# A transformer block with cross-attention: the written-out order of all instructions and the places of its buffers are replaced

## The chip, the cores and the metric

The kernel runs on one core of a Trainium2 chip. The metric is the device time of one execution in microseconds, with all inputs and the output in device memory. Three runs of the kernel before took 652.02, 652.84 and 654.86 us, a median of 652.84.

## The reference

Eight sequences of 256 tokens with 512 features each attend to eight contexts of the same size, with 16 heads of 32 features. All values are f32. A multilayer perceptron with 2048 inner features and the tanh form of gelu follows.

```
x = layer_norm(hidden_states, ln1_w, ln1_b)
q = (x @ q_w + q_b)                      # and split into 16 heads of 32
k = (encoder_hidden_states @ k_w + k_b)
v = (encoder_hidden_states @ v_w + v_b)
scores = where(mask, q k^T / sqrt(32), lowest)
out = softmax(scores) v
hidden = out @ cproj_w + cproj_b + hidden_states
y = gelu(layer_norm(hidden, ln2_w, ln2_b) @ fc_w + fc_b)
return hidden + y @ proj_w + proj_b
```

## The kernel before

The 2048 tokens are worked on in two groups of 1024; a digit 0 or 1 behind a letter in a name (`k1_0`, `o0_1`, `x1`) is the group. The stages of a group are: load and transpose the context (L692-L770); normalise the tokens (`layer_norm`, L793); project to k, v and q (`keys_of`, `values_of`); 16 attention units, one for two head groups and a sequence (`scores` at L1020 and `attend` at L1067); the output projection (`output`, L1410); the multilayer perceptron (`fc`, L1194, and `proj`, L1258).

Every large product is a Strassen-Winograd quad (`quad`, L852): seven products P1, P2, P6, P7, P5, P3, P4 of quarter matrices replace eight. They are written into three PSUM banks called X, Y and W, and between the products another engine reads a bank out (t1, c11, t2, t3, c22, c12, c21). So `k1_0_P7` is the seventh product of the first half of the keys of group 1, and its destination is the bank `k1_0_W`. The sums of quarters that go in (`c1t1`, `kws1`, `fw0i4_1` and so on) are made by VectorE or POOL. All matmuls but the transposes are recorded on one line, L634, so the tile names tell them apart.

An attention unit such as 022 goes like this. TensorE writes the scores s022 into four PSUM banks. ScalarE copies them out in eight pieces (ev022, line L614, tile `pr`), VectorE takes maxima (mx022, L1033), ScalarE moves these together (mc022, L1039), VectorE folds and transposes them (L1040 and mf022, L1042). The result is stored to device memory (md022) and loaded back, broadcast to all partitions (mm022). VectorE (L1053) or POOL (L1057) subtracts it from the two halves of the scores (less022_0, less022_1), ScalarE takes exponentials (L1060), for half of the units VectorE or POOL adds the exponentials in pairs (`ss`, L625), and TensorE multiplies with the values (av022). VectorE inverts the sums (L1083-L1086) and writes the result (att022, L625), which frees the bank of av022.

Nothing in this order is decided while the kernel runs or by a planner in the file. `Order.op` (L54) records each operation with the engines that it may run on and finds what it depends on. `Order.run` (L94) then reads the sequence of issue on all engines from a string, PROGRAM, of 2999 words; a letter behind a word names the engine where there is a choice (V VectorE, A ScalarE, G POOL). Each engine issues its own words in this sequence and never overtakes. All transfers are on the queue of SyncE, also in this sequence, and a transfer that waits for its data holds up those behind it. A second string, PLACES, gives each buffer its slot:

```
for word in PROGRAM.split():
    name, _, e = word.partition(":")
    o = ops.pop(name)
    o.eng = letters[e] if e else o.alts[0][0]
    o.start = len(order)
    order.append(o)
...
where = dict(p.split("=") for p in PLACES.split())
for o in order:
    for b in o.bufs:
        if b.slot is None and b.name in where:
            b.slot = int(where[b.name])
```

The slots are 45 pieces of 1024 f32 for each partition (a piece can serve as two of 512), 14 pieces of 256, small ones, and the eight PSUM banks (kinds W and C). A buffer waits until all users of the one before it in the same slot are done.

Of the kernel before, what the change touches and what calls it, by code (L numbers as in the profile page):

```python
# [122 lines left out]
cq0_00_0 turn_c0_10_0 turn_c0_00_0 vw00 c0_10_0:A c0_00_0:V small v0_0_P1a cq0_00_1 turn_c0_00_1 c0_00_1:A cq0_01_1  # L123
turn_c0_10_1 v0_0_P1b c0_10_1:V v0_1_P1a cq0_01_0 turn_c0_11 cq0_11_0 c0_11:V vw10 cq0_11_1 kw00 vw11 v0_0_t1:A
turn_c0_01 cq0_10_0 cq0_10_1 c0_01:V c0t1:V v0_1_P1b v0_1_t1:A rows1 vws1:V turn_c0_31 turn_c0_21 vws3:G c0_21:A rows7
vws2:G c0_31:A k0_1_P1 xt0_3 vw01 k0_0_P1 rows3 turn_c0_20 c0t2:V fw0_11_0 v0_0_P6 stats_x0_11 c0t3:V vws4:V rows0
turn_c0_30 fw0_11_1 fw0i4_1:G v0_0_t2:A xt0_2 aggr_x0_11 rows2 v0_1_P6 stats_x0_10 c0_20:A aggr_x0_10 kw10 v0_0_P5
rows5 c0_30:A eps_x0_1 v0_0_P2 rows4 rows6 fw0_10_0 c0t4:V v0_1_t2:V v0_0_t3:A pow_x0_1 nb_x0_1 norm_x0_11:A mk kw11
rows8 v0_1_P2 fw0_00_1 v0_0_P3 kws3:V mk~1 fw0i4_3:G fw0_10_1 cols fw0_00_0 xt0_5 v0_1_P5 fw0i4_2:V xt0_6 fw0i4_4:V
kws1:V kws2:V cols~1 k0_0_t1:A k0_1_t1:V xt0_0 k0_1_P6 v0_0_c11 xt0_7 fw0_01_0 fw0s3:V v0_1_t3:A xt0_1 fw0s1:G  # L130
fw0i5_1:G v0_1_c11 stats_x0_31 k0_0_P7 stats_x0_21 k0_1_t2:A fw0i5_2:G kw01 xt0_4 fw0_01_1 fcd0_5_False fcd0_7_False
stats_x0_00 fw0i5_3:V fw0i1_1:V fcd0_4_True fw0i7_1:G fw0i1_3:V k0_0_P6 qw00 k0_0_t2:A aggr_x0_00 fw0i7_2:V fw0i7_4:V
v0_1_P3 fw1_01_0 k0_1_P2 k0_0_P5 fw0i1_2:V fw0s2:V norm_x0_10:A aggr_x0_21 fw1_00_0 qw11 aggr_x0_31 fw0i5_4:V qw01
fw0i1_4:V k0_1_P5 vd0_0_11 stats_x0_01 aggr_x0_01 fw1_01_1 eps_x0_0 v0_1_c12:A kws4:G fw0i7_3:V v0_0_c12:A stats_x0_20
# [12 lines left out]
aggr_x1_11 fold000 q0_1_P5 cb1_00 s020 fw1i5_2:G cb1_02 cb1_13 q0_1_c11 fw1i4_2:V q0_1_t3:A cb1_21 mf000 fw1i3_4:V
q0_1_P3 ev020_21 ev020_20 q0_0_P3 fw1i5_3:G ev020_01 fcd0_3_True eps_x1_1 ev020_30 cb1_10 fw1i7_2:V ev020_31 fw1i5_4:V
fw1i6_1:V ev020_11 mx020_1 ev020_10 ev020_00 fw1i7_3:V fw1i6_2:G mx020_0 q0_1_c12:A q0_1_P7 cT1_10 q0_0_c12:A
fw1i4_4:G cb1_22 fcd1_3_False md000 mc020_2 cT1_00 cT1_11 mc020_1 mc020_3 kd0_0_12 fcd1_7_False pow_x1_1 s002  # L150
fcd1_4_True ev002_10 ev002_11 fold020 mm000 ev002_30 ev002_31 ev002_21 ev002_20 fw1i7_4:V ev002_01 mf020 fw1i3_3:G
v0_0_P7 ev002_00 cT1_01 s022 kd0_1_11 nb_x1_1 v0_1_P7 fw1i6_3:G q0_1_c22 fw1i6_4:G mx002_1 q0_1_P4 fcd1_3_True
ev022_20 mx002_0 v0_1_c22 c1t1:G ev022_30 ev022_21 ev022_31 mx022_1 md020 ev022_10 less000_0:G less000_1:G v0_0_c22
cb1_20 mc002_3 ev022_01 mc002_1 mc002_2 fold002 fcd1_6_False v0_1_P4 ev022_11 mm020 q0_1_c21 v0_1_c21 mf002 ev022_00
v0_0_P4 mx022_0 exp000_0 norm_x1_11:A s010 mc022_3 mc022_1 k1_0_P1 exp000_1 cb1_33 cb1_30 cb1_32 mc022_2 ss000_0:G
cT1_20 cb1_31 v0_0_c21 ev010_30 ev010_11 md002 less020_1:V ev010_00 ev010_21 fold022 ev010_01 ev010_31 fcd1_5_True
ev010_20 ss000_1:G k1_1_P1 kd0_1_22 cT1_21 mf022 ev010_10 less020_0:V av000 s030 exp020_0 cT1_31 cT1_30 norm_x1_10:A
fcd1_6_True md022 k1_1_t1:A xt1_7 ev030_21 ev030_01 mx010_1 ev030_30 xd1_3 r000 att000 k1_0_P2 mx010_0 ev030_00
k1_0_t1:A c1t2:G k1_1_P6 exp020_1 ev030_31 ev030_20 ev030_11 k1_0_c11 mc010_1 mc010_2 mc010_3 c1t3:G kd0_1_12
ss020_0:V ev030_10 kd0_1_21 mm022 xt1_4 k1_0_P6 k1_0_t2:A ss020_1:V xt1_0 av020 stats_x1_31 mx030_1 mx030_0 aggr_x1_31  # L160
fold010 k1_1_t2:A s012 xt1_6 stats_x1_30 ev012_21 fcd1_7_True mc030_2 mc030_1 ev012_31 xt1_1 r020 k1_1_P5 stats_x1_01
att020 mf010 k1_0_P5 mm002 mc030_3 aggr_x1_30 xd1_2 kd0_0_22 k1_0_P7 less022_1:G exp022_1 md010 less022_0:G
stats_x1_00 ev012_20 exp022_0 ss022_0:V ev012_01 vd0_0_21 ku011 less002_1:V ev012_00 k1_0_t3:A mm010 less002_0:V
ev012_30 ev012_11 ev012_10 aggr_x1_01 k1_1_t3:A fold030 vd0_0_12 ss022_1:G av022 c1t4:G exp002_0 s032 vu010 xt1_5
vu030 ev032_30 ev032_11 mf030 aggr_x1_00 k1_0_c22 mx012_1 vd0_1_11 k1_1_P3 ev032_10 ev032_20 ss002_0:G mx012_0 k1_0_P3
ku001 ev032_01 ev032_31 eps_x1_3 eps_x1_0 ev032_00 less010_1:V exp002_1 k1_1_P7 ss002_1:G k1_0_P4 ev032_21 mx032_1
exp010_1 k1_0_c12:A mx032_0 vd0_0_22 stats_x1_20 av002 mc032_2 md030 mc032_3 ku021 mc032_1 k1_0_c21 r022 fold032
att022 mf032 k1_1_c12:A ku003 pow_x1_0 r002 mc012_1 s001 stats_x1_21 mc012_3 att002 k1_1_P2 less010_0:G ss010_1:G
exp010_0 vu011 nb_x1_0 mm030 k1_1_c22 ss010_0:G ev001_11 aggr_x1_21 ev001_31 vu012 pow_x1_3 ev001_30 md032 vu032 ku031
ev001_00 ev001_01 ev001_21 aggr_x1_20 av010 ev001_10 ev001_20 s021 ku023 k1_1_c11 k1_1_P4 norm_x1_01:A eps_x1_2  # L170
# [182 lines left out]
cq0_00=74 cq0_10=32 cq0_01=88 cq0_11=40 ps_cols=7 ps_c0_00_0=6 c0_00=58 ps_c0_00_1=0 ps_c0_10_0=2 ps_c0_10_1=6  # L353
ps_c0_20=7 c0_10=48 ps_c0_30=2 ps_c0_01=2 c0_01=20 ps_c0_11=1 ps_c0_21=2 c0_11=24 ps_c0_31=7 xt0_0=54 xt0_1=6 xt0_2=77
# [105 lines left out]
ps_o11=0 ot1=28 ps_o01=4 ps_o10=7  # L460
# [1053 lines left out]
```

## Time and profile before

| | before |
|---|---|
| median of three runs | 652.84 us (652.02 to 654.86) |
| the profiled execution: its span | 652.0 us (no other time of it is recorded) |
| TensorE, busy | 644.3 us, 99%, 3793 matmuls |
| VectorE, busy | 583.2 us, 89% |
| ScalarE, busy | 346.1 us, 53% |
| POOL, busy | 395.9 us, 61% |
| transfers, share of 16 engines' time | 78.0% |
| granted TensorE clock | 1.000 |

Rows of the profile are read thus. PE is TensorE, DVE is VectorE, ACT is ScalarE, SPq is SyncE's queue, on which a transfer is issued; its data land later. A row of the timeline gives the start, the length, the engine, the line, the operation, the tile written and the tiles read, and in square brackets how long the engine was idle before it and what ended that. Names of tiles are given without their numbers: a buffer in a shared slot can appear under the name of the slot's first user, such as `vw` or `xt`. Matmul ends are modelled, so a stretch that reads as fully busy may hold small gaps.

### The profile page before, as it was taken

Reading aid. Unit: us, or ns where it says so; the run is one execution under the profiler, and the core shown is the slowest. Engines: PE = TensorE matmul, PEld = TensorE weight load, DVE = VectorE, ACT = ScalarE, POOL = GpSimd, SP = SyncE. Lnnn points to the kernel's source line nnn. Section 1 sums busy time; section 2 is a strip of 40 time slices with the busy share of each in tenths; the row PEclk is TensorE's granted clock in tenths of the full one; section 3 lists DMA queues with packets and bytes.
Section 4 is the critical chain, followed back from the end, with each engine's and each line's share of the span. In section 5 each row is a group of like instructions: output and inputs, shape, how many; then the busy total and the mean of one; then the engine's idle time right before and its main releaser. Section 6 shows DMA issues by size and latency. Waiting matters only on the chain.

```text
span 652.0 us, 11225 instructions
## 1 busy us (share of the span) xinstructions
PE 644.3 (99%) x3793; PEld 487.7 (75%) x3793; DVE 583.2 (89%) x985; ACT 346.1 (53%) x709; POOL 395.9 (61%) x351
## 2 busy tenths in 40 slices
PE   9999999999999999999999999999999999999997
PEld 7755463477545776777787888888888888888886
DVE  4989998999999999999999999988878777999975
ACT  2244698999999879966864645220121222523000
POOL 2543675879987897898859756335813265321244
PEclk9999999999999999999999999999999999999999
DMA  8999998778875447787867787897989989677765
GB/s 268 306 328 324 239 251 284 226 204 152 217 224 151 130 168 232 260 267 250 257 214 250 225 272 232 293 314 170 160 222 197 215 198 204 158 190 227 173 138 97
DMA packets 206713, 144.83 MB, mean 222 GB/s; under 512 B 117136, under 2 KB 167104, under 8 KB 206656
## 3 DMA queue, kind: packets, MB, share of 16 engines
q1 hardware_dynamic: 206656, 144.11, 78.0%
q8 instruction: 30, 0.49, 0.3%
q14 instruction: 27, 0.22, 0.1%
HBM read 104.10 MB, written 39.98 MB: 221 GB/s over the span
## 4 chain that ended last, share of the span: by engine, by line
PE 90%; DVE 4%; ACT 2%; issue 1%; DMA 1%; POOL 1%; DVEq 0%
PE pd_X L634 15%; PE fc_X L634 15%; PE fc_W L634 7%; PE pd_W L634 7%; PE av L634 6%; PE q_X L634 4%; PE v_X L634 4%; PE fc_Y L634 4%; PE k_X L634 4%; PE pd_Y L634 4%; PE s L634 4%; PE o_X L634 2%; PE v_W L634 2%; PE k_W L634 2%; PE o_W L634 2%; DVE mx L1033 2%
## 5 line engine op out<-in xcount | busy, mean ns | idle before, releaser
L614 ACT ACTIVATE pr<-s,cols 128x256 f32<-128x256 f32 x256 | 102.9, 485 | 10.7 <-PE s L634 8.2
L1057 POOL TENSOR_TENSOR pr<-pr,mm 128x512 f32<-128x512 f32 x70 | 90.2, 1318 | 7.2 <-DMA xt<-in_x_dram 5.0
L1237 ACT ACTIVATE h<-h,cols 128x256 f32<-128x256 f32 x128 | 55.2, 499 | 61.2 <-DVE h L625 45.2
L1033 DVE TRANSPOSE_TENSOR_REDUCE mx<-pr 128x32 f32<-128x1024 f32 x64 | 76.9, 1216 | 1.5 <-ACT pr L614 1.3
L1060 ACT ACTIVATE pr<-pr 128x1024 f32<-128x1024 f32 x64 | 66.5, 1061 | 12.1 <-POOL pr L1057 9.0
L625 DVE TENSOR_TENSOR h<-fc_X,h 128x512 f32<-128x512 f32 x80 | 52.4, 675 | 5.5 <-PE fc_X L634 4.7
L625 POOL TENSOR_TENSOR ss<-pr 128x512 f32<-128x512 f32 x24 | 31.5, 1325 | 14.2 <-ACT pr L1060 11.8
L625 DVE TENSOR_TENSOR h<-fc_W,h 128x512 f32<-128x512 f32 x48 | 32.0, 677 | 5.0 <-PE fc_W L634 4.4
L1053 DVE TENSOR_TENSOR pr<-pr,mm 128x1024 f32<-128x1024 f32 x29 | 35.2, 1229 | 0.0
L1039 ACT COPY mx<-mx 32x64 f32<-32x64 f32 x96 | 23.2, 243 | 15.9 <-DVE mx L1033 14.7
L623 POOL TENSOR_TENSOR z1t<-h,z1t 128x512 f32<-128x512 f32 x6 | 8.0, 1360 | 26.1 <-PE pd_Y L634 12.3
L625 POOL TENSOR_TENSOR tq<-tq,rq 128x512 f32<-128x512 f32 x8 | 10.1, 1272 | 21.7 <-DMA rq<-hd 15.4
L634 PE MATMUL pd_X<-z0i,pl 128*128 128x256 f32 x96 | 22.5, 379 | 0.0
L634 PE MATMUL fc_W<-y1i,fl 128*128 128x256 f32 x84 | 20.7, 379 | 0.0
L625 DVE TENSOR_TENSOR h<-fc_Y,h 128x512 f32<-128x512 f32 x24 | 15.9, 672 | 5.3 <-PE fc_Y L634 5.3
L634 PE MATMUL pd_W<-z1i,pl 128*128 128x256 f32 x88 | 20.6, 379 | 0.0
L1040 DVE TENSOR_REDUCE mx<-mx 32x32 f32<-32x256 f32 x32 | 18.4, 578 | 2.2 <-ACT mx L1039 2.0
L634 PEld LDWEIGHTS pd_X<-z0i,pl 128*128 128x128 f32 x96 | 18.2, 190 | 2.5
L811 POOL TENSOR_TENSOR rs_y<-rs_y,neg_half 128x2 f32<-128x2 f32 x8 | 10.2, 1289 | 15.3 <-DMA pl<-prd 7.7
L634 PE MATMUL pd_X<-h,pl 128*128 128x256 f32 x80 | 18.9, 379 | 0.0
L601 ACT COPY h<-fc_X 128x512 f32<-128x512 f32 x16 | 9.0, 594 | 18.5 <-PE fc_X L634 15.6
L625 DVE TENSOR_TENSOR po<-pd_X,po 128x256 f32<-128x256 f32 x24 | 9.9, 414 | 9.6 <-PE pd_X L634 9.4
(574 smaller groups left out, 1857.3 us busy)
## 6 DMA issues: line engine op xcount, KB each, us to landing
pl<-prd SPq DMA_DIRECT2D x65, 256.0 KB, 3.7
mm<-md SPq DMA_DIRECT2D x32, 512.0 KB, 4.3
fl<-fcd SPq DMA_DIRECT2D x40, 256.0 KB, 4.5
fw<-in_L_xattn_fc_w_dram SPq DMA_DIRECT2D x16, 256.0 KB, 4.0
hid<-in_x_dram SPq DMA_DIRECT2D x8, 512.0 KB, 5.8
pw<-in_L_xattn_proj_w_dram SPq DMA_DIRECT2D x32, 128.0 KB, 4.1
hd<-hid SPq DMA_DIRECT2D x8, 512.0 KB, 4.9
fcd<-fw0i SPq DMA_DIRECT2D x7, 512.0 KB, 7.1
```

The source lines that it names most:

```text
L601: (nc.scalar.copy if e == "ACT" else nc.vector.tensor_copy)(to(), of_())
L614: lambda e: nc.scalar.activation(to(), of_(), AF.Identity, bias=bias(), scale=1.0))
L625: E[e].tensor_tensor(to(), in0(), in1(), op)
L634: nc.tensor.matmul(o(), l(), r(), start=first, stop=True, skip_group_check=True)
L811: lambda e, rs=rs: nc.gpsimd.tensor_tensor(tile_of(rs)[:, 2:4], tile_of(rs)[:, 0:2], neg_half[:, 0:2], ALU.pow), lock=True)
L1033: T.op(f"mx{u}_{h}", [("DVE", 1.126)], [(pr[h], None)], [(mx, [h])], lambda e, h=h: nc.vector.tensor_reduce(tile_of(mx)[:, 0:64].rearrange ...
L1039: lambda e, a=a: nc.scalar.copy(tile_of(mx)[0:32, 64 * a : 64 + 64 * a], tile_of(mx)[32 * a : 32 * a + 32, 0:64]))
L1040: T.op(f"fold{u}", [("DVE", 0.38)], [(mx, [0, 1, 2, 3, 4])], [(mx, [5])], lambda e: nc.vector.tensor_reduce(tile_of(mx)[0:32, 256:288], ti ...
L1053: nc.vector.tensor_tensor(p_, p_, m_[:, None, :].to_broadcast([P, 2, 512]), ALU.subtract)
L1057: E[e].tensor_tensor(p_, p_, m_, ALU.subtract)
L1060: lambda e, h=h: nc.scalar.activation(tile_of(pr[h]), tile_of(pr[h]), AF.Exp), table="exp")
L1237: lambda e, f=f, b=b, c=c: nc.scalar.activation(at(h[f][b], c), at(h[f][b], c), AF.Gelu_apprx_tanh, bias=col(c_fcb + f * 4 + c), scale=1.0 ...
```

## The change

Only the two strings differ. PROGRAM has the same 2999 operations in another sequence on every engine, and 167 operations stand on another one of their allowed engines: of the words with a letter, VectorE has 252 instead of 261, POOL 270 instead of 254, ScalarE 134 instead of 141. PLACES gives 1029 of 1304 buffers another slot or bank. No operation is added or removed, and the code that makes the instructions is the same.

```diff
--- before.py
+++ after.py
@@ -120,344 +120,344 @@
 PROGRAM = """
-cq0_00_0 turn_c0_10_0 turn_c0_00_0 vw00 c0_10_0:A c0_00_0:V small v0_0_P1a cq0_00_1 turn_c0_00_1 c0_00_1:A cq0_01_1
...
-ss020_0:V ev030_10 kd0_1_21 mm022 xt1_4 k1_0_P6 k1_0_t2:A ss020_1:V xt1_0 av020 stats_x1_31 mx030_1 mx030_0 aggr_x1_31
...
-att020 mf010 k1_0_P5 mm002 mc030_3 aggr_x1_30 xd1_2 kd0_0_22 k1_0_P7 less022_1:G exp022_1 md010 less022_0:G
...
-ev132_11 ev132_30 ev132_31 o0_0_c12 exp102_0 o0_1_t3 ev132_01 fold112 pw0_10_11 exp122_1 o0_0_P7 att100 mf112 mm130
...
+cq0_00_0 small turn_c0_10_0 turn_c0_00_0 c0_00_0:V cq0_00_1 vw00 turn_c0_00_1 turn_c0_10_1 c0_10_0:A v0_0_P1a
...
+mx010_1 r000 k1_1_t1:A exp020_0 exp020_1 c1t2:G k1_0_c11 c1t3:G mm022 less022_1:G k1_1_P6 k1_0_P6 norm_x1_10:A
...
+k1_0_P7 mc030_1 less002_0:V k1_0_t3:A exp002_0 k1_1_P5 xt1_1 stats_x1_01 md010 xt1_4 ss022_1:G av022 vu030 mm010 xt1_5
...
+ev132_00 ev132_10 md130 md110 pw0_11_01 mm130 pw0_10_11 o0_0_P7 mx132_0 less120_0:G ev132_31 ev132_20 ev132_30 o0_1_P7
...
 """
...
 PLACES = """
...
-mm010=4 ss010=4 av020=3 r020=1 rc020=4 att0_10=88 vu030=10 s030_0=3 s030_1=5 s030_2=6 s030_3=4 pr030_0=8 pr030_1=10
...
-c1t4=24 x1t1=6 x1t2=66 x1t3=48 x1t4=46 k1_0_X=2 k1_0_11=35 k1_0_Y=7 k1_0_21=65 k1_0_W=3 k1_0_22=41 k1_0_12=60 k1_1_X=1
...
-rc122=1 att1_11=48 s132_0=1 s132_1=0 s132_2=5 s132_3=7 pr132_0=4 pr132_1=66 mx132=2 mm132=80 av110=1 r110=3 rc110=3
...
-o0_0_X=6 o0_0_Y=1 o0_0_W=7 o0_1_X=4 o0_1_Y=5 o0_1_W=2 st_y0_0=2 mv_y0_0=0 rs_y0_0=9 xn_y0_00=68 xn_y0_01=38 st_y0_1=3
...
+mm010=4 ss010=4 av020=5 r020=6 rc020=0 att0_10=88 vu030=3 s030_0=5 s030_1=3 s030_2=0 s030_3=7 pr030_0=8 pr030_1=10
...
+c1t4=24 x1t1=14 x1t2=62 x1t3=50 x1t4=46 k1_0_X=2 k1_0_11=35 k1_0_Y=6 k1_0_21=65 k1_0_W=7 k1_0_22=41 k1_0_12=60
...
+rc122=0 att1_11=48 s132_0=3 s132_1=0 s132_2=7 s132_3=1 pr132_0=4 pr132_1=6 mx132=0 mm132=82 av110=6 r110=8 rc110=7
...
+o0_0_X=4 o0_0_Y=3 o0_0_W=5 o0_1_X=6 o0_1_Y=1 o0_1_W=3 st_y0_0=5 mv_y0_0=3 rs_y0_0=9 xn_y0_00=81 xn_y0_01=11 st_y0_1=9
...
 """
```

Three places show what the strings do. The first is on TensorE, in the key projection of group 1, round unit 022. All rows are matmuls; `s012` are scores of another unit. Before:

```order
L634 MATMUL s012_3_1107<-q0_1_21_742,qw00_460 128x256
L634 MATMUL k1_1_X_985<-c1t1_900,kws1_405 128x512 x2
L634 MATMUL k1_0_X_956<-c1t1_900,kws1_405 128x512 x2
L634 MATMUL k1_0_W_1142<-c1t3_1062,xt0_3_297 128x512 x2
L634 MATMUL av022_1176<-ss022_1154,ones_89 32x256 x4
L634 MATMUL av022_1176<-pr022_0_909,v0_0_22_369 32x256 x2
```

After the change:

```order
L634 MATMUL s012_3_1119<-q0_1_21_747,xt0_5_517 128x256
L634 MATMUL k1_0_X_990<-c1t1_906,kws1_343 128x512 x2
L634 MATMUL k1_0_W_1168<-c1t3_1057,kws1_343 128x512 x2
L634 MATMUL k1_1_X_999<-c1t1_906,kws1_343 128x512 x2
L634 MATMUL av022_1182<-ss022_1160,ones_89 32x256 x4
L634 MATMUL av022_1182<-pr022_0_883,xt0_7_378 32x256 x2
```

The product `k1_0_W` (P7) stood last ahead of av022, and now stands one product earlier, with `k1_1_X` behind it. The table of places moves `k1_0_W` from bank 3, which av020 holds until att020 is done, to bank 7; av020 moves to bank 5, where av022 is as well.

The second place is SyncE's queue, from the stores of the maxima of units 002 and 022 (md, read from mx) to the broadcast load mm022. The other rows are copies of weights sums, keys and tokens (fcd, kd, xd) to device memory and loads of keys and tokens. Before:

```order
L594 DMA md002_146<-mx002_891 32x32
L594 DMA fcd1_5_106<-fw1i5_752 128x2x512
L594 DMA kd0_1_22_127<-v0_0_22_369 128x512
L594 DMA fcd1_6_107<-fw1i6_804 128x2x512
L594 DMA md022_147<-mx022_906 32x32
L588 DMA k1_1_11_1025<-in_x_dram 128x512
L594 DMA xd1_160<-xn_x1_11_940 128x512
L594 DMA kd0_1_12_125<-qw00_460 128x512
L594 DMA kd0_1_21_126<-k0_1_21_440 128x512
L588 DMA mm022_1070<-md022_147 128x1024
```

After the change:

```order
L594 DMA xd1_160<-xn_x1_11_957 128x512
L588 DMA xt1_6_980<-in_x_dram 128x512
L594 DMA kd0_1_12_125<-xt0_5_517 128x512
L588 DMA v0_1_21_335<-in_x_dram 128x512
L594 DMA md022_147<-mx022_922 32x32
L588 DMA ku011_1005<-kd0_1_11_124 128x256
L594 DMA md002_146<-mx002_891 32x32
L594 DMA fcd1_3_104<-fw1i3_856 128x2x512
L588 DMA mm022_1060<-md022_147 128x1024
```

The store md022 now stands ahead of md002 instead of behind it, and another set of transfers stands between it and mm022.

The third place is TensorE in the output projection of group 0. `o0_0` and `o0_1` are the two halves, s132 the scores of a unit of group 1. Before:

```order
L634 MATMUL s132_3_2482<-qws2_639,xn_x1_11_940 128x256
L634 MATMUL o0_1_X_2299<-ows1_1955,a0t1_2284 128x256 x4
L634 MATMUL o0_1_W_2510<-xt0_7_419,a0t3_2307 128x256 x4
L634 MATMUL o0_0_W_2525<-xt0_7_419,a0t3_2307 128x256 x4
L634 MATMUL o0_1_Y_2537<-k0_0_11_411,att0_10_1131 128x256 x4
```

After the change:

```order
L634 MATMUL s132_3_2478<-qws2_670,xt0_5_517 128x256
L634 MATMUL o0_1_X_2288<-ows1_1956,a0t1_2284 128x256 x4
L634 MATMUL o0_0_W_2515<-vw10_244,a0t3_2323 128x256 x4
L634 MATMUL o0_1_W_2528<-vw10_244,a0t3_2323 128x256 x4
L634 MATMUL o0_1_Y_2546<-v0_1_22_478,att0_10_1162 128x256 x4
```

The two products P7 into W have changed places. The table of places moves `o0_0_W` from bank 7 to 5 and `o0_1_W` from bank 2 to 3; the scores s132 lie in banks 1, 0, 5, 7 before and in 3, 0, 7, 1 after.

654 lines of the change are left out of this document (327 added, 327 removed).

## The prediction

> **What bounds the kernel now.** The page's first and fourth parts come first: busy time by engine, and the chain that ended last.
>
> ```profile
> PE 644.3 (99%) x3793; PEld 487.7 (75%) x3793; DVE 583.2 (89%) x985; ACT 346.1 (53%) x709; POOL 395.9 (61%) x351
> PE 90%; DVE 4%; ACT 2%; issue 1%; DMA 1%; POOL 1%; DVEq 0%
> ```
>
> TensorE has work for 644.3 of 652.0 us and is nine tenths of the chain. The change leaves its matmuls as they are, so only its idle time can move, 7.7 us by this row. The busy time by stretch of 20 us says where that lies (the first two columns are the stretch's length and PE's busy time with its count; behind the other engines come granted clock, DMA share and GB/s).
>
> ```profile
> 0.00:20.00 20.00, 19.02 (x106) 15.38 (x107) 10.41 (x16) 5.84 (x10) 6.10 (x13) 1.00 0.83 262
> 40.00:60.00 20.00, 20.00 (x72) 10.57 (x71) 16.90 (x28) 9.38 (x14) 11.93 (x14) 1.00 1.06 355
> 80.00:100.00 20.00, 20.00 (x133) 12.22 (x126) 19.63 (x33) 17.72 (x41) 15.19 (x13) 1.00 0.96 257
> 100.00:120.00 20.00, 18.50 (x111) 8.25 (x110) 17.48 (x32) 16.99 (x37) 12.16 (x10) 1.00 0.88 286
> 140.00:160.00 20.00, 19.82 (x185) 14.06 (x185) 19.20 (x32) 19.42 (x44) 17.24 (x14) 1.00 0.77 153
> 180.00:200.00 20.00, 19.89 (x136) 9.23 (x138) 19.64 (x30) 19.62 (x40) 15.81 (x10) 1.00 0.78 244
> 200.00:220.00 20.00, 19.82 (x196) 12.39 (x189) 19.65 (x33) 19.02 (x44) 17.73 (x13) 1.00 0.29 81
> 220.00:240.00 20.00, 18.99 (x132) 14.74 (x131) 19.84 (x31) 15.21 (x39) 18.12 (x15) 1.00 0.45 148
> 300.00:320.00 20.00, 19.73 (x176) 14.30 (x168) 19.62 (x38) 17.19 (x30) 15.87 (x14) 1.00 0.79 245
> 400.00:420.00 20.00, 20.00 (x94) 17.60 (x94) 19.74 (x30) 7.69 (x18) 7.45 (x6) 1.00 0.78 255
> 640.00:652.00 12.00, 8.50 (x51) 7.42 (x49) 5.34 (x12) 0.00 (x0) 2.74 (x2) 0.98 0.52 104
> ```
>
> The idle time is 0.98 at the start, 3.50 behind the last matmul, and 3.25 us in between (1.50 + 0.18 + 0.11 + 0.18 + 1.01 + 0.27), all of it before 320 us: in the attention stages, where VectorE too is busy for 19 of 20 us. From 400 us on a stretch is full, 94 matmuls in 20 us, and can only get worse. TensorE's waits by releaser name the same places:
>
> ```profile
> PE k_W L634 <- DVE mx L1042: 1.5, 1, 1.5
> PE o_W L634 <- ACT pr L614: 1.0, 1, 1.0
> PE first L646 <- DVE warm L641: 1.0, 1, 1.0
> PE av L634 <- ACT pr L614: 0.3, 1, 0.3
> ```
>
> So two places hold 2.5 of the 3.25 us. The rest of the prediction asks what becomes of these two, and whether the new order makes another.
>
> **The wait at 233 us.** The timeline (start, length) round the product `o0_0_P7`:
>
> ```profile
> 232.38 1.89 PE L634 MATMUL o_W<-xt,a0t 128*128 128x256 f32 x8
> 234.02 1.20 ACT L614 ACTIVATE pr<-s,cols 128x256 f32<-128x256 f32 x3
> 235.28 0.48 PE L634 MATMUL o_W<-xt,a0t 128*128 128x256 f32 x1 [1.01 <-ACT pr L614]
> ```
>
> Eight matmuls of `o0_1_P7` end at 234.27; the next eight need PSUM bank 7, which still holds one of the four score banks of unit s132, and ACT's last copies out of it run to 235.22. In the new table the pair stands the other way round: first `o0_0_P7` into bank 5, which s132 does not use, then `o0_1_P7` into bank 3, which two of the eight copies of s132 have to free, while one more product of 1.89 us runs. Bounds: the whole 1.0 saved, or nothing, if those two copies are the late ones. The cover of 1.89 us is longer than the wait; I take **-1.0**.
>
> **The wait at 109 us, and what is late behind it.**
>
> ```profile
> 105.61 4.95 POOL L1057 TENSOR_TENSOR pr<-pr,mm 128x512 f32<-128x512 f32 x4 [4.96 <-DMA xt<-in_x_dram]
> 107.84 0.70 DVE L802 BATCH_NORM_STATS2 st_x<-xt 128x6 f32<-128x512 f32 x1 [2.08 <-DMA xt<-in_x_dram]
> 110.36 0.41 DVE L625 TENSOR_TENSOR att<-av,r 128x256 f32<-128x256 f32 x1
> 110.60 1.06 ACT L1060 ACTIVATE pr<-pr 128x1024 f32<-128x1024 f32 x1 [1.04 <-POOL pr L1057]
> 110.91 1.95 PE L634 MATMUL k_W<-c1t,xt 128*128 128x512 f32 x4 [1.50 <-DVE mx L1042]
> 111.69 0.69 DVE L625 TENSOR_TENSOR ss<-pr 128x512 f32<-128x512 f32 x1 [0.17 <-ACT pr L1060]
> 112.80 0.64 PE L634 MATMUL av<-ss,ones 128*32 128x256 f32 x8
> ```
>
> VectorE stands still for 2.08 us at a statistics instruction whose tokens land late; the multiplication att020 that empties bank 3 is queued behind it and ends at 110.77; then `k1_0_P7` may write bank 3. The table of places puts that product into bank 7 now, so this wait goes. But that is not yet 1.5 us. The next product is av022. Its probabilities wait for the broadcast maximum mm022: POOL subtracts it from 105.61, the second exponential ends at 111.66, the half sum at 112.38, and av022 starts at 112.80. Without the wait TensorE would be there at 111.3, and stand until 112.4: the saving is 0.4 us, unless mm022 lands earlier. This is where the queue of SyncE comes in:
>
> ```profile
> 94.32 0.16 DVE L1042 STREAM_TRANSPOSE mx<-mx 32x32 f32<-32x32 f32 x1
> 94.77 0.61 SPq L594 DMA_DIRECT2D md<-mx  x1
> 98.31 0.43 SPq L588 DMA_DIRECT2D mm<-md  x1
> mm<-md SPq DMA_DIRECT2D x32, 512.0 KB, 4.3
> ```
>
> The load is issued at 98.31, and POOL starts as soon as it has landed, about 7 us later, against a median of 4.3. Two things move it. Counted over the instructions in front of it (lengths as traced), VectorE reaches this transposition with 3.1 us less work, and the order has md022 before md002 instead of behind it: up to 3.1 us earlier. On SyncE 116 transfers stand in front of mm022 instead of 109; with the sizes of each, ten more and three fewer are 1.31 MB, which at the highest rate in the windows above (355 GB/s at a share of 1.06) are 3.7 us: up to 3.7 us later. The windows of 80 to 120 us show shares of 0.96 and 0.88, so the queue had some 20 x 0.10 + 5 x 0.18 = 2.9 us to spare before the landing, in which most of the extra 3.7 can go. Net about 2 us earlier to 0.6 us later. Bounds of the whole place: -1.5, where mm022 keeps pace, and +3.7 - 0.4 = +3.3, where the queue delays it fully. Nearest to the spare share I take **-0.8**.
>
> **Start and constants.** The first key weights become the tenth large load instead of the ninth; 256 KB at 355 GB/s are 0.74 us. The value products that stand in front of the first key product are mostly there earlier, so I take **+0.3** (bounds -0.3 and +0.7). The constants' transposition is moved ahead of two value products:
>
> ```profile
> 17.95 0.36 SPq L588 DMA_DIRECT2D rows<-in_L_xattn_proj_b_dram  x1
> 26.66 0.27 PE L682 MATMUL ps_cols<-ident,rows 64*128 64x64 f32 x1
> ```
>
> It ran 8.7 us after the last of its loads was issued. Two products of 1.89 us fewer in front put it at about 22.9; the last load stands three large transfers further back, at 20.2, and needs a few us to land: bounds 0 and +1.5, taken **+0.3**.
>
> **Engines exchanged.** VectorE has 9 operations fewer, ScalarE 7 fewer, POOL 16 more. None of them is on TensorE; they are covered as long as POOL's chains keep their places. The rows that price them:
>
> ```profile
> L1057 POOL TENSOR_TENSOR pr<-pr,mm x70: 1258/1274/2279, 84.9 to 312.7; 128x512 f32<-128x512 f32 x70
> L1053 DVE TENSOR_TENSOR pr<-pr,mm x29: 1171/1216/1564, 92.1 to 368.7; 128x1024 f32<-128x1024 f32 x29
> ```
>
> A subtraction is 2 x 1.27 us on POOL and 1.22 on VectorE. less020, less030 and less032 have one half each moved to POOL, 1.33 us more in a chain; but the two halves in POOL's row follow each other, where before one waited for VectorE, and POOL is idle for 2.8 of 20 us by the row of 140 to 160 us. Taken as 0, bounds -0.5 and +2.7 (two units in a row). The Trainium skill ("SBUF — State Buffer", SBUF: two separate sides) says that VectorE with two SBUF inputs and a GpSimd operation that reads SBUF exclude each other for a whole instruction. The trace has a median of 1274 beside a minimum of 1258 and a VectorE that is almost always busy, so most of the 70 were not held up, though one was by a microsecond; by the rule the moved halves would cost up to a VectorE instruction each, which is a rival below.
>
> **Small waits.** 0.74 us of the 3.25 are neither place (0.18 + 0.11 + 0.18 + 0.27). They hang on this very order and mostly go; others will come in their place, and I take **-0.3**.
>
> **Sum.** -1.0 - 0.8 + 0.3 + 0.3 + 0 - 0.3 = -1.5: a span of 650.5 instead of 652.0. The runs' median is 652.84, 0.84 above the profiled span, so 651.3 is the forecast. Measurement can tell half a per cent, 3.3 us, from no change: faster means under 649.6, slower over 656.1.
>
> **Rivals.**
> (a) *Nearly every wait goes.* Then the 3.25 us go whole, and something at the start: 652.84 - 3.25 - 0.5 = 649.1; gaps that the records hide as longer matmuls (1.89 for eight here) could give another 1 to 2, so 648.3. For it: all waits have one named cause each, and VectorE is lighter by about 3 us at the critical place. Against it: VectorE is still busy for 19 of 20 us, so each chain has under a microsecond to spare.
> (b) *Waits are exchanged one for one.* av022 takes over all that `k1_0_P7` loses, and s132's copies are late for `o0_1_P7`: 652.8. For it: av022 started 0.42 us behind its sum.
> (c) *The maxima are late behind SyncE's queue (slower).* At 80 to 120 us the DMA share is near its highest. In front of mm020 stand 1.70 MB more, in front of mm002 1.83 MB, 4.8 and 5.2 us at 355 GB/s. If the spare share is not to be had, since SyncE stands at stores that wait for VectorE, TensorE waits at av020, av022 and av002 for the largest of these once: 652.84 - 1.0 + 5.2 + 0.6 (start) = 657.6. It decides from about 3.5 us of lateness on; below that the earlier maximum and the 0.4 us cover it. Against it: 2.9 us spare. The Trainium skill ("DMA: Bandwidth & Descriptors", Queues, rings and completion order) has each DMA engine consume one queue's descriptors in order, which by itself would speak for (c); no row here shows whether a small store is let past.
> (d) *POOL's chain becomes the bound at 125 to 145 us.* Two units with 1.33 us more each, and by the port rule a VectorE instruction of 1.22 for each of six half subtractions: 651.3 + 2.7 + 6 x 0.6 = 657.6 where every second one is held up. For it only the longest of 2279 ns; against it the median.
>
> **How the numbers follow.** Forecast (within 1.5 us of 651.3) 0.35, (a) 0.31, (b) 0.12, (c) 0.15, (d) 0.07. Faster is (a), 0.31; slower (c) and (d), 0.22; same the rest, 0.47. The range reaches down to 647.2, past (a)'s centre by a microsecond, and up to 656.8, which holds the halves of (c) and (d) where only part of the lateness comes through; some 0.2 is left outside. The forecast's own range is 649.8 to 652.8.
>
> **What would show it.** Right: no wait of an o_W or k_W matmul above 0.3 us in TensorE's waits; the window of 220 to 240 us at 19.8 or more; a wait of 0.3 to 1 us on an av at 109 to 113 us; PE's busy time again 644 to 645. (a): all windows from 20 to 320 us at 19.9 or more. (b): av in place of k_W with 1 to 1.5 us. (c): av waiting on POOL's or VectorE's subtraction, this on a DMA, with 3 us or more at 95 to 125 us. (d): av waiting on POOL's half sum, and a median of L1057 above 1.4 us. The prediction is wrong if one wait of over 2 us stands at a place that is not named here, above all behind 400 us, where there was nothing to gain.

## The result: 5.7 per cent slower

Four runs of the changed kernel took 689.69 to 693.91 us, a median of 692.08, against 653.85 for the kernel before on the same chip. The ratio of the means is 1.0574, with a 95% interval of 1.0533 to 1.0614: 37.5 us more on 653.85. The forecast was 651.3 us, in a range of 647.2 to 656.8. One execution of e14, an experiment below, took 1357 us, twice its three others, and is left out of its ratio.

### The profile page after: what moved, and what is told of

Read it like the earlier page. It is cut to its first block, busy times and chain, and to the rows that moved or that the text cites. A ratio compares the mean times of both kernels' runs of the same rounds, so it can differ in the third digit from the quotient of the medians.

```text
span 692.1 us, 11191 instructions
## 1 busy us (share of the span) xinstructions
PE 657.4 (95%) x3793; PEld 488.7 (71%) x3793; DVE 597.0 (86%) x976; ACT 340.9 (49%) x702; POOL 441.8 (64%) x379
## 4 chain that ended last, share of the span: by engine, by line
PE 32%; DVE 7%; DMA 7%; SPq 3%; issue 1%; POOL 1%; POOLq 0%; DVEq 0%
PE pd_X L634 10%; PE fc_X L634 8%; PE pd_W L634 5%; PE fc_W L634 4%; SPq L588 3%; PE pd_Y L634 2%; DMA pl<-prd 2%; PE fc_Y L634 2%; DVE h L625 1%; DMA fl<-fcd 1%; DMA rq<-hd 1%; DMA xt<-prd 1%; DVE a1t L625 1%; DMA out_dram<-tq 1%; DVE pw1s L625 1%
## 5 line engine op out<-in xcount | busy, mean ns | idle before, releaser
L1057 POOL TENSOR_TENSOR pr<-pr,mm 128x512 f32<-128x512 f32 x76 | 96.8, 1301 | 12.8 <-DMA mm<-md 12.7
L625 DVE TENSOR_TENSOR h<-fc_X,h 128x512 f32<-128x512 f32 x80 | 52.2, 675 | 16.4 <-PE fc_X L634 15.5
L625 POOL TENSOR_TENSOR ss<-pr 128x512 f32<-128x512 f32 x23 | 31.5, 1379 | 11.9 <-ACT pr L1060 8.3
L625 DVE TENSOR_TENSOR h<-fc_W,h 128x512 f32<-128x512 f32 x48 | 31.8, 675 | 2.7 <-PE fc_W L634 2.6
L1039 ACT COPY mx<-mx 32x64 f32<-32x64 f32 x96 | 23.1, 242 | 16.9 <-DVE mx L1033 9.7
L811 POOL TENSOR_TENSOR rs_y<-rs_y,neg_half 128x2 f32<-128x2 f32 x8 | 14.2, 1782 | 16.3 <-DVE rs_y L808 16.2
L623 POOL TENSOR_TENSOR z1i<-h,z1i 128x512 f32<-128x512 f32 x10 | 13.1, 1332 | 16.6 <-DVE z1i L625 13.7
L1428 POOL TENSOR_TENSOR hid<-hid,cb 128x1024 f32<-128x1024 f32 x6 | 16.6, 2786 | 9.7 <-DMA hid<-in_x_dram 9.7
L623 POOL TENSOR_TENSOR z1t<-h,z1t 128x512 f32<-128x512 f32 x8 | 13.8, 1744 | 14.1 <-DVE z1t L625 11.2
L634 PE MATMUL pd_W<-z0i,pl 128*128 128x256 f32 x88 | 20.9, 380 | 0.4 <-issue 0.4
L634 PE MATMUL fc_X<-y1t,fl 128*128 128x256 f32 x60 | 16.0, 400 | 4.9 <-DMA fl<-fcd 4.9
L634 PE MATMUL fc_W<-y1i,fl 128*128 128x256 f32 x72 | 18.4, 380 | 0.8 <-DVE po L625 0.8
L601 ACT COPY h<-fc_X 128x512 f32<-128x512 f32 x15 | 8.7, 585 | 21.3 <-PE fc_X L634 21.2
L634 PEld LDWEIGHTS pd_W<-z1i,pl 128*128 128x128 f32 x88 | 16.6, 190 | 3.4 <-issue 1.1
L634 PEld LDWEIGHTS pd_W<-z0i,pl 128*128 128x128 f32 x88 | 16.6, 190 | 3.0 <-issue 0.8
```

Of the source, the lines that this page charges most:

```text
L623: nc.gpsimd.tensor_tensor(to()[:, ts(k, 512)], in0()[:, ts(k, 512)], in1()[:, ts(k, 512)], op)
L625: E[e].tensor_tensor(to(), in0(), in1(), op)
L634: nc.tensor.matmul(o(), l(), r(), start=first, stop=True, skip_group_check=True)
L1039: lambda e, a=a: nc.scalar.copy(tile_of(mx)[0:32, 64 * a : 64 + 64 * a], tile_of(mx)[32 * a : 32 * a + 32, 0:64]))
L1057: E[e].tensor_tensor(p_, p_, m_, ALU.subtract)
```

## The profile after

The first part and the head of the fourth part of the changed kernel's page (busy time by engine; shares of the chain that ended last):

```profile
PE 657.4 (95%) x3793; PEld 488.7 (71%) x3793; DVE 597.0 (86%) x976; ACT 340.9 (49%) x702; POOL 441.8 (64%) x379
PE 32%; DVE 7%; DMA 7%; SPq 3%; issue 1%; POOL 1%; POOLq 0%; DVEq 0%
```

TensorE is idle for 34.7 of 692.1 us where it was idle for 7.7. That is 27.0 of the 40.1 us by which the profiled span grew. The other 13.1 us stand in TensorE's busy time, 657.4 instead of 644.3 us for the same matmuls: small gaps that the records of the matmuls cover, and a granted clock of 0.992 (0.997 in the three other runs) instead of 1.000, which on 657 us would be some 5 us, an estimate. TensorE's waits by releaser, the longest of a list of 28 rows:

```profile
PE fc_X L634 <- DMA fl<-fcd: 6.3, 2, 4.9
PE s L634 <- DVE att L625: 2.3, 2, 2.0
PE k_X L634 <- ACT k L606: 1.8, 1, 1.8
PE av L634 <- DVE mx L1042: 1.7, 1, 1.7
PE pd_X L634 <- DMA xt<-prd: 1.6, 1, 1.6
PE o_X L634 <- DVE hid L625: 1.5, 1, 1.5
```

The two waits of before, of k_W at 109 us and of o_W at 233 us, are gone as the prediction had it. The full list sums to 30.4 us instead of 3.8: 15.5 for VectorE, 11.3 for transfers, 3.2 for ScalarE, 0.4 for nothing that is named. No single wait is the cause; the only one clearly over 2 us is the 4.9 of the first row. By stretches of 20 us (length, then busy time with count of PE, PEld, DVE, ACT, POOL, then granted clock, DMA share, GB/s):

```profile
20.00:40.00 20.00, 18.22 (x64) 11.67 (x64) 14.78 (x34) 3.62 (x6) 12.16 (x13) 1.00 1.04 270
160.00:180.00 20.00, 17.28 (x108) 12.94 (x112) 17.32 (x25) 16.24 (x36) 18.84 (x16) 0.98 0.75 132
220.00:240.00 20.00, 18.04 (x112) 11.91 (x105) 19.52 (x35) 16.03 (x41) 14.28 (x13) 0.91 0.23 81
400.00:420.00 20.00, 18.20 (x82) 14.80 (x80) 19.93 (x24) 6.81 (x17) 13.56 (x10) 1.00 0.40 134
520.00:540.00 20.00, 15.09 (x63) 12.67 (x63) 13.56 (x29) 1.18 (x2) 9.02 (x12) 0.91 0.96 196
```

The loss is spread over the whole span, the part behind 400 us included, which had been full before. Following each TensorE operation in both traces and subtracting the steady length of all matmuls in front of it gives TensorE's lag:

| TensorE's own work done (us) | 60 | 160 | 260 | 380 | 480 | all |
|---|---|---|---|---|---|---|
| lag before (us) | 5.9 | 10.1 | 14.6 | 16.7 | 16.8 | 17.1 |
| lag after (us) | 11.8 | 24.8 | 34.3 | 44.7 | 56.1 | 57.3 |

**VectorE's instructions are longer.** Its busy time grew by 13.8 us, from 583.2 to 597.0, though it has nine instructions fewer. Matched by name, the instructions that are on VectorE in both kernels (its common instructions, below) take 18.7 us longer. The smallest show it best. These are the rows of lines L808 and L814, on 128x2 elements (lengths in ns: min/median/max). Before:

```profile
L808 DVE TENSOR_SCALAR rs_y<-mv_y x8: 135/160/169, 246.2 to 427.3; 128x2 f32<-128x2 f32 x8
L814 DVE SCALAR_TENSOR_TENSOR rs_x<-mv_x,rs_x x8: 107/149/194, 21.0 to 132.0; 128x2 f32<-128x2 f32 x8
```

After:

```profile
L808 DVE TENSOR_SCALAR rs_y<-mv_y x8: 134/164/2022, 261.6 to 454.6; 128x2 f32<-128x2 f32 x8
L814 DVE SCALAR_TENSOR_TENSOR rs_x<-mv_x,rs_x x8: 159/678/1300, 36.5 to 143.3; 128x2 f32<-128x2 f32 x8
```

The same instruction takes 0.16 us or up to 2.02. The timeline of the changed kernel at the longest one (start, length):

```profile
259.87 3.76 POOL L1057 TENSOR_TENSOR pr<-pr,mm 128x512 f32<-128x512 f32 x3
...
261.63 2.02 DVE L808 TENSOR_SCALAR rs_y<-mv_y 128x2 f32<-128x2 f32 x1
```

It ends at 263.65, where POOL's three subtractions end at 263.63: VectorE stands until POOL lets go, past the end of one POOL instruction (at 262.4) and through the next. Such an instruction is called held up here. Counting every VectorE instruction that is more than 0.2 us over the shortest tenth of its kind gives 27 with 16.9 us too much before, and 55 with 41.6 us after; of these 10.7 and 34.4 us lie before 430 us. So the change adds 24 us of hold-ups to an engine that was already busy for 17 to 20 of every 20 us there (from 20 us on).

Not every kind is held up. By the same count it happens to sums, differences and products of two tensors, and to some that work on one tensor (TENSOR_SCALAR). It never happens to VectorE's transpositions, reductions and statistics, such as the 64 maxima of the changed kernel:

```profile
L1033 DVE TRANSPOSE_TENSOR_REDUCE mx<-pr x64: 1190/1211/1247, 75.1 to 374.9; 128x32 f32<-128x1024 f32 x64
```

The Trainium skill ("SBUF — State Buffer", SBUF: two separate sides) states an exclusive lock, held for the whole instruction, between a GpSimd operation and a VectorE instruction that has two SBUF inputs (if the GpSimd operation reads SBUF) or runs in what it calls a 2-port perf mode. The trace agrees as to the instructions with two inputs; in which mode an instruction like L808, with one input, ran is in no row here. The trace also shows that a held-up instruction can miss the gap between two instructions of the other engine.

POOL has long instructions too. By the same count they went from 43 with 31.0 us to 53 with 43.3 us. The longest is in this row:

```profile
L811 POOL TENSOR_TENSOR rs_y<-rs_y,neg_half x8: 687/1382/6146, 263.7 to 455.2; 128x2 f32<-128x2 f32 x8
```

Lengths on POOL are rough in the profile, and what made these long was not tested.

## The experiments

All were measured beside runs of the kernel before on the same chip. Ratios are against it; the change itself has 1.0574.

### Undoing one part: five kernels that mix two layouts

The two strings allow a mixture: letters of one with the sequence of the other (e1, e2), the start of one with the rest of the other (e3, e4), and only SyncE's row of transfers exchanged (e6). As an example, a word of e1 against before; e2 sets the same word back in the change:

```diff
-less030_0:V
+less030_0:G
```

> The sequence and the places of before; only the 167 operations that the change puts on another engine are put there. Theory P (the exchanged engines bring POOL and VectorE into each other's way): 665 to 685 us, the 128x2 operations of VectorE (lines L808, L814), at most 194 ns before, reach 1 us or more. Theory S (an early slip: VectorE loses 8 us to late loads in the first 35 us, and all that was timed behind it falls apart) and theory D (the new sequence is bad in every stage by itself): 650 to 657 us.

> The sequence and the places of the change, but every operation on the engine that it had before. Theory P: 655 to 670 us. Theories S and D: 683 to 697 us, since the engines matter little.

> The operations that start in the first 60 us of before in before's sequence and engines, all others in the change's; 35 of 1304 buffers get another free slot where the two tables clash. Theory S: the slip is not made, 650 to 660 us. Theory D: only the 6 us that TensorE's lag differs at 60 us are saved, 683 to 688 us. Theory P: as D.

> The other way round: the operations that start in the first 60 us of the change in its sequence and engines, all others in before's; 88 buffers get another slot. Theory S: 670 to 695 us, since the slip of VectorE is made and before's sequence was timed as closely. Theory D: before and the 6 us of the first 60 us, 656 to 661 us.

> Before's sequence, engines and places, only SyncE's transfers stand in the change's sequence as nearly as the data and the places allow (a transfer is 2.3 places off the change's on average, before's are 10.2 off). Theory L (late transfers start it): 670 to 690 us, with VectorE waiting for loads before 40 us as in the change and TensorE for weights at 460 to 535 us. Theories B and P: 651 to 658 us.

| | median (us) | ratio | 95% interval |
|---|---|---|---|
| e1, before with the change's engines | 702.21 | 1.0721 | 1.0680 to 1.0762 |
| e2, the change with before's engines | 722.63 | 1.1006 | 1.0935 to 1.1078 |
| e3, before until 60 us, then the change | 704.19 | 1.0746 | 1.0704 to 1.0789 |
| e4, the change until 60 us, then before | 685.11 | 1.0452 | 1.0384 to 1.0520 |
| e6, before with the change's transfers | 915.16 | 1.3968 | 1.3895 to 1.4041 |

No theory had this pattern: e1, e2, e3 and e6 are slower than every theory said. Theory S (an early slip of VectorE starts everything) falls as the cause of the change's loss: e3 has before's first 60 us, TensorE's lag there is 5.5 us (5.9 before), and it ends slower than the change. But e4 lies in the range that theory S gave it: TensorE's lag at 60 us is some 12 us above before's there, the whole loss is about 30 us, and VectorE's common instructions are only 5.8 us longer. So under before's sequence a late start costs more than itself; 88 other places in e4 may have a part in that.

Theory P falls as far as it needs the exchanged engines: e2 has before's engines, and VectorE's common instructions are 33.4 us longer than before. It does not fall as a part of the cause: in e1, with the change's engines in before's sequence, they are 8.3 us longer, and by the count above, which takes in the instructions that the exchange moved, some 50 are held up for 36 us, 18 of them before 430 us. So either the engines or the sequence alone makes hold-ups; what counts is which instruction stands beside which.

Beyond that the five say little about the change, since each mixture is slower than the layouts that it was made from or lies between them. e1 and e4 lose 47 and 30 us with 18 and 14 us of hold-ups before 430 us, where the kernel before has 11, so a sequence in a setting that it was not made for loses time in other ways too. e6 shows it at its worst; the first part of its page, and TensorE's longest waits:

```profile
PE 705.3 (78%) x3793; PEld 515.0 (57%) x3793; DVE 594.9 (66%) x985; ACT 346.7 (38%) x709; POOL 392.4 (43%) x351
```

```profile
PE fc_X L634 <- DMA fl<-fcd: 27.8, 2, 14.1
PE pd_W L634 <- DMA pl<-prd: 22.2, 2, 15.4
PE pd_X L634 <- DMA pl<-prd: 15.9, 2, 12.4
```

### The places: e5

```diff
-k1_0_W=3 o0_0_W=7 av020=3
+k1_0_W=7 o0_0_W=5 av020=5
...
```

(and 431 more banks and small slots)

> Before's sequence and engines; the PSUM banks and the small slots (434 of 1304 buffers) are those of the change, save 83 that clash; the large slots stay. Theory B (places: a product or a copy waits for another user of its bank): 665 to 700 us, with waits of TensorE on reads out of banks. Theory V (VectorE, full until 430 us, is delayed by other things: by POOL at the shared port, by late loads): 651 to 660 us.

The ratio was 1.0132 (1.0101 to 1.0163), 8.6 us; VectorE's common instructions were as long as before (0.0 us of difference). Between the two expectations: other banks under the same sequence cost something, but a quarter of the change's loss and none of its hold-ups. The large slots were not tried, since the change's do not fit before's sequence.

### What a late VectorE costs: e7, e8, e14, e15, and POOL: e16

```diff
 for o in order:
     o.fn(o.eng)
+    if o.name in late:
...
+        for _ in range(3):
+            nc.vector.transpose(spare, ident.t)
```

(e14 and e15; e7 and e8 have 34 transpositions behind one operation, e16 two fills on POOL in place of the three)

> Before, with 34 useless transpositions of 128x128 (about 8 us) on VectorE at 62 us. Theory V: VectorE has no time to spare until 430 us, so TensorE ends later by 8 us or more: 660 to 672 us. Theory T (TensorE alone sets the time, as the prediction had it): at most 3 us, 652 to 656 us.

> The same 34 transpositions at 450 us, where VectorE is busy for 14 to 17 of 20 us. Theory V: the delay is made up for within 50 us, 652 to 657 us. A theory by which each operation stands just in time, whatever the load: 660 us or more as in the run before.

> Before, with 24 delays of VectorE of three transpositions each (about 1.0 us, 25 us in all), evenly spread from 40 to 430 us: as many and as long as the hold-ups that the change adds there (24 us). Theory S (sum: each hold-up is paid, since VectorE has no spare time there and TensorE waits for it within a microsecond): 672 to 680 us. Theory N (a microsecond is hidden, only long delays reach TensorE): 653 to 660 us.

> The same 24 delays from 440 to 640 us, where VectorE is busy for 13 to 19 of 20 us. Theory S with spare time: part of it is hidden, 656 to 668 us. Theory N: 653 to 657 us. If every operation stands just in time there too: 674 us or more.

> Before, with 24 delays of POOL of two fills of 128x512 each (about 1.05 us, which read nothing), from 40 to 430 us, where POOL is busy for 7 to 19 of 20 us. If POOL's chains have room: 653 to 657 us. If they stand just in time as well: 660 to 675 us.

| | delay put in (us) | ratio | 95% interval | paid (us, of 653) |
|---|---|---|---|---|
| e7, VectorE, one at 62 us | 11.8 | 1.0188 | 1.0146 to 1.0231 | 12.3 |
| e8, VectorE, one at 450 us | about 11.7 | 1.0203 | 1.0170 to 1.0236 | 13.3 |
| e14, VectorE, 24 from 40 to 430 us | 21.8 | 1.0325 | 1.0303 to 1.0347 | 21.2 |
| e15, VectorE, 24 from 440 to 640 us | 22.1 | 1.0129 | 1.0108 to 1.0149 | 8.4 |
| e16, POOL, 24 from 40 to 430 us | 25.3 | 1.0152 | 1.0129 to 1.0175 | 9.9 |

The delay put in is the sum of the added instructions in the trace for e14 to e16, and the stretch from the first to the last of them for e7 and e8. The first row gives it for e14, the second for e7:

```profile
L1478 DVE STREAM_TRANSPOSE spare<-ident 128x128 f32<-128x128 f32 x72 | 21.8, 303 | 1.7
```

```profile
L1476 DVE STREAM_TRANSPOSE spare<-ident x34: 301/312/313, 63.3 to 74.8; 128x128 f32<-128x128 f32 x34
```

In e7 TensorE pays most of it at one place, on a read by VectorE; of the second wait 1.5 us stood in the profile of before:

```profile
PE q_W L634 <- DVE vws L625: 10.1, 1, 10.1
PE k_W L634 <- DVE mx L1042: 2.1, 1, 2.1
```

So theory T, the prediction's picture of TensorE alone setting the time, is wrong: a long delay of VectorE is paid whole, even at 450 us, where VectorE is idle for some of every 20 us and where theory V had expected it to be made up for (652 to 657 us; the median is 668.03). A likely reason, not tested, is that this room cannot be used in advance: in the profile of before VectorE's idle time there is spent on waits for TensorE's products. In e7 and e8 the granted clock is lower as well, 0.992 and 0.991, which may be part of what they pay.

Small delays are what tells the two regions apart. Before 430 us 24 of them, together nearly as long as the hold-ups that the change adds, are paid almost whole: 21.2 us for 21.8 put in and 3.4 by which VectorE's other instructions grew. Behind 440 us 8.4 us are paid for 22.1 and 6.3. In e16 9.9 us are paid for 25.3 on POOL, but VectorE's instructions are 11.9 us longer there, so this run does not tell a late POOL from a VectorE that POOL holds up. A delay of a microsecond need not stand out among TensorE's longest waits: e14's list begins

```profile
PE o_X L634 <- DVE a1t L625: 2.8, 1, 2.8
PE q_W L634 <- DVE att L625: 1.7, 1, 1.7
PE av L634 <- DVE h L625: 1.5, 2, 1.1
```

which is as spread as the change's.

### Taking the hold-ups away: e9 and e10

```diff
+    def silent(to, a, b, op):
+        nc.gpsimd.tensor_tensor(to[..., ::128], a[..., ::128], b[..., ::128], op)
+        for _ in range(2):
+            nc.gpsimd.memset(to, 0.5)
...
-                    E[e].tensor_tensor(p_, p_, m_, ALU.subtract)
+                    silent(p_, p_, m_, ALU.subtract)
```

(the second place is L1057; L623 and L625 call it likewise where the engine is POOL)

> The change, but each sum, difference and subtraction on POOL (L623, L625, L1057) is replaced by a tensor operation on every 128th column and two fills of the same region, which read nothing and together take about as long; so these values are left out of the computation. The waits for the operands stay. Theory P (VectorE is held up while a POOL operation reads its operands: 34 us before 430 us in the change, 11 in before): VectorE's 128x2 operations stay under 0.3 us, and the time falls by 15 to 30 us more than that of before does in the next run: 660 to 675. Theory N (the hold-ups cost nothing, since other work is late anyway): 685 to 693 us.

> The control: before, with the same replacement (the same values left out). Theory P: 645 to 654 us, as there is little to gain. Theory N: 650 to 656 us. If the fills take longer or shorter than the operations that they replace, both runs show it in the same way.

The ratios were 1.0514 (1.0474 to 1.0553) and 1.0168 (1.0115 to 1.0222). The first parts of both pages, of e9 and then of e10:

```profile
PE 655.5 (95%) x3793; PEld 490.0 (71%) x3793; DVE 564.1 (82%) x976; ACT 340.1 (49%) x702; POOL 441.4 (64%) x1077
```

```profile
PE 649.5 (98%) x3793; PEld 487.5 (73%) x3793; DVE 570.4 (86%) x985; ACT 346.7 (52%) x709; POOL 403.9 (61%) x993
```

and in e9 the 128x2 instructions of VectorE, whose lines are seven further down there:

```profile
L815 DVE TENSOR_SCALAR rs_y<-mv_y x8: 145/164/170, 257.5 to 450.5; 128x2 f32<-128x2 f32 x8
L821 DVE SCALAR_TENSOR_TENSOR rs_x<-mv_x,rs_x x8: 107/154/163, 36.0 to 137.8; 128x2 f32<-128x2 f32 x8
```

Of the 16 others on these two lines one took 0.60 us.

Where POOL hardly reads, VectorE's work is 32.9 us shorter in the change (597.0 to 564.1) and 12.8 us shorter in before (583.2 to 570.4). That shows where the hold-ups come from: from POOL's reads. The time followed only in part. The change became 3.9 us faster, within intervals that overlap, and the control 11.0 us slower. The replacement (0.30 and twice 0.53 us, with gaps) is a little longer than the 1.27 us that it stands for, and that a later POOL costs time is the likely reason for the slower control. Against the control the change gained 14.9 us for 20.1 us of hold-ups, with an uncertainty of some 5 us (an estimate from the three intervals). Without most of VectorE's hold-ups the two layouts are still 22.6 us apart instead of 37.5, so the larger part of the loss has other causes. The times that theory P gave were missed for both, e9 (660 to 675) and e10 (645 to 654), as it had left the longer replacement out; its difference of 15 to 30 us was met at its lower edge.

### One queue of loads: e11, and two early ones: e12

```diff
-... fl112_0 rq0_22 pl04_4 ... fl106_2 ... fl116_3 fl116_0 ...
+... fl112_0 pl04_4 ... fl106_2 ... fl116_3 fl116_0 ... fl107_2 rq0_22 ...
```

> The change, but eight of the sixteen loads rq0 (00 to 03 and 20 to 23), whose users come at 553 us or later, are issued behind fl107_2 instead of among the weights of fc1; four of them stood ahead of fl116_0, for which TensorE waits 5.1 us at 531 us. Theory L (that wait is the queue in front of it, and is paid in full): 3 to 5 us less, 687 to 689 us. If another load takes its place: 691 to 693 us.

> The change, but two early loads are moved ahead of three that are needed later: xt0_7 (VectorE waits 2.8 us for it at 24 us) and fw0_10_0 (2.3 us at 32 us, with the chain to k0_1_t1 and TensorE's 1.9 us at 38.6 us behind it). Theory L: each wait of VectorE there is paid in full, 2 to 6 us less, 686 to 690 us. If the lateness is only pushed on to the next load: 691 to 694 us.

Five of the loads rq0 change their place; the other three that the expectation names stood behind fl107_2 already. e11: 1.0460 (1.0415 to 1.0506), 7.4 us less than the change; the two intervals allow about 3.5 to 11, so this is not told apart from the 3 to 5 expected. The row of the change that names the wait, from its timeline, and TensorE's wait for the same tiles in e11:

```profile
531.15 2.07 PE L634 MATMUL fc_X<-y1t,fl 128*128 128x256 f32 x4 [4.91 <-DMA fl<-fcd]
```

```profile
PE fc_X L634 <- DMA fl<-fcd: 1.2, 1, 1.2
```

Four loads that nobody needed for 20 us stood ahead of one that TensorE was to need next.

e12: 1.0561 (1.0522 to 1.0600), not told apart from the change. VectorE's waits before 60 us, in the change and then in e12:

```profile
DVE st_x L802 <- DMA xt<-in_x_dram: 2.8, 1, 2.8
DVE fw0s L625 <- DMA fw<-in_L_xattn_fc_w_dram: 2.3, 1, 2.3
```

```profile
DVE st_x L802 <- DMA xt<-in_x_dram: 1.9, 2, 1.7
DVE fw0s L625 <- DMA fw<-in_L_xattn_fc_w_dram: 1.6, 1, 1.6
...
DVE st_x L802 <- DMA v<-in_x_dram: 0.6, 1, 0.6
```

The two waits shrank by 1.6 us, and another load took 0.6 of it: lateness pushed on.

### The two waits that the prediction counted as a gain: e13

```diff
-k1_0_W=3 av022=5 o0_0_W=7 o0_1_Y=5
+k1_0_W=5 av022=3 o0_0_W=5 o0_1_Y=7
```

> Before, with only four buffers in other banks: k1_0_W in 5 and av022 in 3 (they change places), o0_0_W in 5 and o0_1_Y in 7 (likewise). These are the two terms of the prediction alone. As it had them: no wait of o_W at 235 us (-1.0), the wait of k_W at 109 us gone but av022 waiting for its half sum instead (-0.4): a span of 650.4 to 650.8 and 0.2 per cent less. If the waits are worth their full length: 649.5. If something behind them takes the time: no change.

The ratio was 1.0018 (0.9998 to 1.0038). TensorE's longest waits:

```profile
PE first L646 <- DVE warm L641: 1.0, 1, 1.0
PE ps_c L722 <- DMA cq<-in_ctx_dram: 0.9, 1, 0.9
PE q_W L634 <- DVE att L625: 0.9, 1, 0.9
PE s L634 <- DVE att L625: 0.7, 1, 0.7
```

Both waits are gone, and the time is not less. New ones of 0.4 to 0.9 us stand at 190 to 215 us (q_W, s). Most of them also stand in the profile of e8, which is the kernel before up to 450 us, so part of this is the difference between two executions of one kernel. The same holds for one of the two waits. In e8 they read

```profile
PE o_W L634 <- ACT pr L614: 1.0, 1, 1.0
PE k_W L634 <- ACT pr L614: 0.2, 1, 0.2
```

and in e15, which is the kernel before up to 440 us, they are the same. So the 1.5 us of k_W belong to the one execution that was read, and only o_W was there to be gained; a gain of its 1.0 us would still lie outside the interval.

## Why the prediction was wrong

**What bounds the kernel.** "Only its idle time can move, 7.7 us" read TensorE's 99% as the bound and looked for what its two named waits would become. The idle time is now 34.7 us, and the busy time, which was to stay at 644 to 645, is 657.4. All but one of the windows quoted from 80 to 420 us had VectorE at 19 to 20 of 20 us, and the text used that only to say that no chain has much to spare. e7 and e14 show what that means: until 430 us a microsecond of VectorE is nearly a microsecond of the kernel. A list of TensorE's waits says what is left after a layout has been fitted; it is no bound on what another layout adds. The upper end of the range was made from three named places, and the loss is spread over many small ones.

**The wait at 233 us, -1.0, and the wait at 109 us, -0.8.** The mechanism was right in the trace of the change and in e13: both waits went. Their worth was not: together 0 within 0.2 per cent in e13. The one at 109 us was read from a single execution, and stands at 0.2 us in e8 and e15, which do the same up to there; where the other stood, other waits stand now. (In rival (a), 649.1 less 1 to 2 us is 647.1 to 648.1, not 648.3; nothing hangs on it.)

**SyncE's queue.** Rival (c) had late loads for the attention at 95 to 125 us. There TensorE's lag grows by about as much as before. The loads that cost something were others: weights of the perceptron behind 460 us, above all at 531 us, where e11 gives back 7.4 us by issuing some other loads (rq0) later. The prediction's own sign of being wrong, a wait of over 2 us behind 400 us, stands there with 4.9. It said of that part that it can only get worse and put no number on it; behind 380 us of TensorE's own work the lag grows by 12.6 us (44.7 to 57.3), before by 0.4.

**Start and constants, +0.6.** The lag at 60 us is 5.9 us larger than before, and VectorE is idle for 8 us more by then. The prediction looked at TensorE's first operands and the constants, not at VectorE's first loads, behind which it stood for 5.1 us.

**Engines exchanged, 0.** This is the step that failed most. It priced the moved operations on POOL's chains by their own lengths, and took from POOL's median of 1274 ns that most instructions are not held up. That median is the same after (1273), but it says nothing of VectorE, whose hold-ups went from 16.9 to 41.6 us. They are worth 15 to 20 us (below), against bounds of -0.5 and +2.7. The term also looked at the moved operations alone, while the new sequence makes hold-ups with before's engines too (e2). Rival (d) had the mechanism, but at six subtractions at 125 to 145 us and with POOL as the one that is late, at a chance of 0.07.

**What adds up, and what stays open.** Of 37.5 us e11 accounts for 7.4, and the hold-ups for 15 (by e9 against e10) to about 20 (24 us at the rate that e14 paid, 21.2 for 25.2). Both are estimates with some 5 us of uncertainty. That leaves 10 to 15 us for the rest: VectorE's late start, of which e12 recovered nothing, the other places and banks (8.6 us in before's sequence by e5), a POOL that is late itself, the granted clock, and operations that simply come in an order in which their inputs are not ready, as in e1 and e4. These were not told apart. Why this sequence has more collisions than the one before is not shown either; e1 and e2 show that engines and sequence each make some.

## What to carry to other kernels

When two engines are both busy for 95% of a stage, price a new order by what it does to each of them, and take a microsecond of either as a microsecond of the whole until a delay put in on purpose shows otherwise. Look for instructions far longer than the shortest of their kind: their engine may be paying for a neighbour's, and no list of waits names it. Read a wait of a microsecond in more than one execution before counting on it. A laid-out order is one piece: undoing half of it measures the mixture and not the half.

## What the runs showed of the hardware that was not expected

A VectorE instruction on 128x2 elements, 0.16 us at the median, took up to 2.02 us beside POOL's subtractions, and stayed under 0.2 us in that row of e9, where POOL filled the same region without reading much. The 64 maxima on VectorE, of 1.21 us each, were not lengthened in the same stretch (1.25 at most). TensorE's granted clock falls with its waits, and not by their sum: 0.91 in a stretch with one wait of 4.9 us (520 to 540 us), 1.00 in one with 1.8 us of small ones (400 to 420 us), and 0.898 over the whole of e6, where single waits reach 15 us. The Trainium skill ("TensorE: Matmul & The Clock Gate", HAM oscillation — how this bites in real kernels) puts the limit at gaps of about 3.4 us; the first two agree. The changed kernel's windows at 0.93 (180 to 200 us) and 0.91 (220 to 240 us) do not: the longest waits there are 1.7 us, which ends at 179.65, and 2.0 us, which ends at 223.63.
